# Bilinear sampling in a fused two-layer convolution: where the transposed source blocks come from

## The chip, the cores and the metric

One core of one Trainium2 chip runs the whole program. Its engines are named as in the profile: PE (TensorE, matrix multiplication, with PEld for its weight loads), DVE (VectorE), ACT (ScalarE), POOL (GpSimd) and SP (SyncE, which only issues DMAs here). The metric is the device time of one execution in microseconds; lower is better.

## The reference

The input has 32 images of 96 channels and 56 x 56 pixels, all in float32. Layer 0 expands to 576 channels, applies a 3 x 3 depthwise convolution, squeeze-and-excite and a projection back to 96 channels, and adds its input. Layer 1 gates that result by channel and by pixel to y, and samples y at learned offsets. The part that this document is about, cut to what matters:

```
y = x * ca * sa
offset = _conv(aux, off_w, off_b, (1, 1))      # aux: y, 4 coordinates, a frequency map
y_base = _conv(y, base_w, base_b, (1, 1))
px, py = xx + off[:, :, 0], yy + off[:, :, 1]  # 9 taps for every pixel
sampled = _grid_sample_taps(y, px, py)         # bilinear, zero outside
y_def = jnp.einsum('bcthw,oct->bohw', sampled, def_w.reshape(c, c, 9)) + def_b
z = (1 - gate) * y_base + gate * y_def         # then batch norm over all images, + x, relu
```

## The kernel before, in words

The images go through three stages that overlap: `hidden` (layer 0 up to the depthwise convolution, stored to `h2d`), `attend` (projection from `h2d` with the `hq` loads of L307 and the matmuls of L323, spectra, and the two gates `ca` and `sa`), and the sampling of an image. The main loop of `layers` walks the sampling in 224 bands of 8 rows, 7 for each image. While the bands of image b run, the generator `attend` of image b+1 and `hidden` of image b+2 are advanced step by step (`pump`), so that their work lies between that of the sampling. A band has 17 slots: one for each of its 14 tiles of 4 columns and three at its end. Work that must come some slots later is put into the list `later` with a slot number, and `pump` calls it then.

The gated image stands in one buffer `yp` in SBUF (channels on partitions, two rows and columns of padding). It is refilled for image b+1 row by row behind the bands of image b: `refill` loads 38 rows at band 5 (`turn`), and more at the ends of bands 5 and 6; `attend_rows` multiplies by the gates four slots later.

Sampling works on tiles of 4 x 4 pixels. All bilinear taps of such a tile lie in a source block of 8 x 8 pixels (offsets are bounded by a check at the end). For each half of a band (h = 0, 1; 7 tile columns, two tiles above each other) the kernel needs

- the weights: `offsets` makes them one or two bands ahead. Its offsets go from `at` to DRAM (`od`, POOL, L634), come back spread over 112 partitions (`ht`, SP, L646), are turned to hat functions on ACT (L649, held at its place in the program, and L650), and are stored as `hd` (ACT's queue, L653). `weights_load` then loads, on SP, the column factors `wc` and the row factors `wr` of a half, each as two DMAs of 64 partitions x 4,032 bytes whose source has an outer dimension of 8 (a broadcast of 8 copies or 8 rows), L664 and L665. `weights` multiplies them on DVE (L671). `prepare` loads one half ahead of the multiplication.
- the source blocks with pixels on partitions: `block_channels` copies the 14 blocks of 8 x 8 pixels out of `yp` on POOL (L682, two copies), transposes them one tile column at a time on PE (L686, seven transposes of 96 x 128), and copies the two PSUM banks to `yt` on ACT (L688, two copies).

`sample_tiles` multiplies block by weights (L700, 28 matmul records for a half, in a group of 3 and one of 4 tile columns), ACT copies the result to `v` (L704), `pack` moves taps 7 and 8 under the others (L711, three copies), and `deform` applies the 3 x 3 kernel (L719) after the first group of the next half.

SP issues its DMAs in the order of the program. The order on the other engines is worked out by the compiler from the dependencies and its own estimate of times, apart from instructions that are held at their place. Every DMA of SP and of ACT's queue signals on one of 8 semaphores taken in turn, so that the ninth DMA waits until the first has landed.

Of the kernel before, what the change touches and what calls it, by code (L numbers as in the profile page):

```python
# [7 lines left out]
FP = mybir.dt.float32  # L8
# [8 lines left out]
C, H, W = 96, 56, 56  # L17
# [3 lines left out]
RB = 8  # L21
# [9 lines left out]
PD = 2  # L31
HY, WY = H + 2 * PD, W + 2 * PD
# [4 lines left out]
TS = 4  # L37
NTX = W // TS
NTH = NTX // 2
TP = TS * TS  # L40
GROUPS = ((0, 3),), ((3, 5), (5, 7))
REACH = PD
SB = TS + 2 * REACH
NS = SB * SB
KP = NTAP * TP
BC = 64
# [16 lines left out]
AHEAD = 1  # L63
READY = 1
# [50 lines left out]
def bank(p):  # L115
    return p["mm"].tile([128, 512], FP, name="mm")
# [441 lines left out]
def load_rows(nc, p, yp, b, x1, r0, r1):  # L558

    rows = yp[:C, PD + r0 : PD + r1, PD : PD + W]  # L560
    nc.sync.dma_start(rows, x1.rearrange("c (h w) -> c h w", h=H)[:, r0:r1])
    sab = p["q2"].tile([C, RB, W], FP, name="sab")[:, : r1 - r0]
    nc.gpsimd.dma_start(sab, p["sa", b].rearrange("o (h w) -> o h w", h=H)[:, r0:r1].to_broadcast([C, r1 - r0, W]))
    return rows, sab


def attend_rows(nc, p, b, rows, sab):

    nc.vector.scalar_tensor_tensor(rows, rows, p["ca", b], sab, ALU.mult, ALU.mult)
# [49 lines left out]
def offsets(nc, p, yp, j, top, hids, ybs, hds):  # L619
# [22 lines left out]
    for _ in range(4):  # L642
        yield
    ht = p["ht"].tile([SB * NTX, 4, KP], FP, name="ht")
    src = od.rearrange("t s o p -> t (s o p)").unsqueeze(0).to_broadcast([SB, NTX, 4 * KP])
    nc.sync.dma_start(ht.rearrange("q n k -> q (n k)"), src)  # L646
# [4 lines left out]
    yield  # L651
    hd = p["dp"].tile([4, SB, NTX, KP], FP, name="hd")
    nc.scalar.dma_start(hd.rearrange("x i t n -> (i t) x n"), ht)  # L653
# [3 lines left out]
def weights_load(nc, p, hd, h):  # L657

    src = hd.rearrange("n i t k -> n i (t k)")[:, :, h * NTH * KP : (h + 1) * NTH * KP]
    wc = p["wc"].tile([2 * NS, NTH * KP], FP, name="wc")  # L660
    wr = p["wr"].tile([2 * NS, NTH * KP], FP, name="wr")
    for s in range(2):
        ps = slice(s * NS, (s + 1) * NS)
        nc.sync.dma_start(wc[ps], src[2 * s].unsqueeze(0).to_broadcast([SB, SB, NTH * KP]))  # L664
        nc.sync.dma_start(wr[ps], src[2 * s + 1].unsqueeze(1).to_broadcast([SB, SB, NTH * KP]))  # L665
    return wc, wr


# [3 lines left out]
    return wc  # L672


def block_channels(nc, p, yp, j, h):

    yt = p["yt"].tile([2 * NS, NTH, C], FP, name="yt")
    yb = p["ybl"].tile([C, NTH, 2, SB, SB], FP, name="ybl")
    src = yp[:C, j * RB : j * RB + SB, h * NTH * TS : h * NTH * TS + SB]
    for s in range(2):  # L680
        blocks = bass.AP(src.tensor, src.offset + s * TS * WY, [src.ap[0], [TS, NTH], [WY, SB], [1, SB]])
        nc.gpsimd.tensor_copy(yb[:, :, s], blocks)  # L682
    for lo, hi in ((0, 4), (4, NTH)):
        pt = bank(p)
        for t in range(lo, hi):
            nc.tensor.transpose(pt[:, (t - lo) * C : (t - lo + 1) * C], yb[:, t].rearrange("c s r x -> c (s r x)"),  # L686
                                p["w"]["ident"][:C, :C])
        nc.scalar.copy(yt[:, lo:hi].rearrange("p t c -> p (t c)"), pt[:, : (hi - lo) * C])  # L688
    return yt


def sample_tiles(nc, p, yt, s, v, group):
# [3 lines left out]
    for (lo, hi), pt in zip(group, pts):  # L696
        for t in range(lo, hi):
            for k in range(2):
                ps = slice(k * NS, (k + 1) * NS)
                nc.tensor.matmul(pt[k][:C, (t - lo) * KP : (t - lo + 1) * KP], yt[ps, t], s[ps, t * KP : (t + 1) * KP],  # L700
# [174 lines left out]
    w["thT"], w["twT"], w["tv"], w["thM"] = thT, twT, tv, thM  # L875


def padded(nc, p, a, images):

    cp = p["cp"]  # L880
    yps = [cp.tile([CJ, HY, WY], FP, name=f"yp{i}") for i in range(images)]
    for t in yps:
        nc.gpsimd.memset(t, 0.0)
        nc.sync.dma_start(t[C : C + 4, PD : PD + H, PD : PD + W], a["coord"])
        nc.sync.dma_start(t[CA:, PD : PD + H, PD : PD + W], a["place"])
    p["s4"] = [cp.tile([H, 3, WP], FP, name=f"s4_{i}") for i in range(2)]
    for t in p["s4"]:
        nc.gpsimd.memset(t, 0.0)
    return yps
# [8 lines left out]
def layers(tc, a, dp, x1d, zd, stats, far):  # L898
# [6 lines left out]
    nc = tc.nc  # L905
    B = x1d.shape[0]
    with ExitStack() as ctx:
        p = {"tc": tc, "dp": ctx.enter_context(tc.tile_pool(name="l1d", bufs=3, space=DRAM))}
        pools(tc, ctx, p, PSUM, (("mm", 6), ("acc", 1), ("pd", 1)))
        hidden_constants(tc, ctx, a, p)  # L910
        constants(tc, ctx, a, p)
        yp, = padded(nc, p, a, 1)
        top = p["cp"].tile([NOFF, NBD + 1], FP, name="top")
        nc.gpsimd.memset(top, 0.0)
        pools(tc, ctx, p, None, (("xt", 2), ("acch", 2), ("pl", 2), ("w3s", 1), ("hq", 9), ("o", 2), ("x2", 3),
                                 ("ca", 2), ("s1p", 1), ("xc", 2), ("sp", 1), ("sq", 1), ("q1", 2), ("q2", 2), ("hid", 3), ("yb", 4),
                                 ("off", 1), ("st", 2), ("ht", 1), ("wc", READY + AHEAD + 1), ("wr", AHEAD + 1), ("yt", 2), ("ybl", 1),
                                 ("vp", 2)))

        def first(b):  # L920
# [13 lines left out]
        streams, later = [], []  # L934
        slot = 0

        def flush():
            while later:
                later.pop(0)[1]()

        held = {}
        count = lambda it: sum(1 for _ in it)
# [5 lines left out]
        due = 0.0  # L948
# [38 lines left out]

        filled = {}

        def refill(b, upto):  # L990

            upto = min(H, upto)
            r = filled.get(("y", b), 0)
            while ("sa", b) in p and r < upto:
                r1 = min(upto, r + RB)
                args = load_rows(nc, p, yp, b, x1d[b], r, r1)
                later.append((slot + 4, lambda args=args: attend_rows(nc, p, b, *args)))
                r = filled["y", b] = r1
            r = filled.get(("fq", b), 0)
            if ("fq", b) in p and r < upto:  # L1000
                load_freq(nc, p, yp, b, r, upto)
                filled["fq", b] = upto
# [21 lines left out]
        def fill():  # L1024
            for r in range(RB, H + 1, RB):
                refill(0, r)
                flush()
                yield

        for _ in beside(fill()):  # L1030
            pass
        bands = [(b, j) for b in range(B) for j in range(NBD)]
        hids, ybs, hds, ready = [], [], [], []

# [8 lines left out]
        flush()  # L1043
        p.pop("diag")
        n_loads = 0
        loads = []

        def prepare(upto):

            nonlocal n_loads  # L1050
            while n_loads < min(upto, 2 * len(hds)):
                n, m = divmod(n_loads, 2)
                loads.append(weights_load(nc, p, hds[n], m))
                n_loads += 1

        prepare(READY + AHEAD)
        for _ in range(READY):
            ready.append(weights(nc, *loads.pop(0)))
        yts = [block_channels(nc, p, yp, 0, 0)]
        start(0, turn * (NTX + 2))  # L1060
        for n, (b, j) in enumerate(bands):
            if j == 0:
                st = p["st"].tile([C, NBD, 6], FP, name="st")
            if j == turn:
                drain()
                refill(b + 1, j * RB - PD)
                flush()
                start(b + 1, slots)
            more = find(n + 2) if n + 2 < len(bands) else iter(())
            next(more, None)  # L1070
            for h in range(2):
                v = p["vp"].tile([128, NTAP, NTH, 2, TP], FP, name="v")
                prepare(2 * n + h + READY + AHEAD)
                s = ready.pop(0)
                yt = yts.pop(0)
                for i, group in enumerate(GROUPS):
                    sample_tiles(nc, p, yt, s, v, group)
                    for _ in range(group[0][0], group[-1][1]):
                        next(more, None)
                        pump()  # L1080
                    if i == 0:
                        for end in ends:
                            end()
                        ends.clear()
                        if h == 1 and n + 1 < len(bands):
                            yts.append(block_channels(nc, p, yp, bands[n + 1][1], 0))
                        ready.extend(weights(nc, *ws) for ws in loads[:1])
                        del loads[:1]
                        if h == 0:
                            yts.append(block_channels(nc, p, yp, j, 1))  # L1090
                pack(nc, v)
                if h == 0:
                    gate = gate_of(nc, p, hids[n])
                ends.append(lambda n=n, h=h, v=v, gate=gate, st=st: end_half(n, h, v, gate, st))
            for _ in more:
                pass
            pump()
            pump()
            pump()
            if b + 1 < B:  # L1100
                refill(b + 1, (j + 1) * RB - PD if j < NBD - 1 else H)
            if j == NBD - 1:
                nc.vector.tensor_reduce(top[:, NBD:], top, AX.X, ALU.max)
# [4 lines left out]
        every = p["cp"].tile([NOFF, 1], FP, name="every")  # L1108
# [344 lines left out]
```

## Time and profile before

| quantity | value |
|---|---|
| time, median of 3 runs (lowest to highest) | 9753.98 us (9741.36 to 9758.91) |
| the profiled execution: its span, the only time the page gives of it | 9792.0 us |
| PE, DVE, ACT, POOL busy | 90%, 74%, 55%, 27% of the span |
| mean granted TensorE clock | 0.937 |
| DMA traffic | 1485.54 MB in 1,085,590 packets |
| share of the 16 DMA engines: SP's queue q1, ACT's queue q10, POOL's q0 | 39.0%, 9.1%, 6.3% |

The span runs from the first to the last instruction and is 38 us (0.4%) longer than the median of the runs. Group rows of the profile read: line, engine, operation, out<-in by the names of the program, shapes, count, then busy time in us and mean ns of one, then idle time of the engine just before them. A matmul in float32 has two records; a transpose has one. A mean on PE is the time from start to end of one record, which overlap; what one adds to the path is less.

### The profile page before, as it was taken

To read this page: it belongs to the slowest core of one execution; us is meant where nothing else is said; L and a number is where in the kernel's file an instruction comes from. 1 tells how busy PE (TensorE), PEld (TensorE's weight loads), DVE (VectorE), ACT (ScalarE), POOL (GpSimd) and SP (SyncE) were. 2 spreads that over 40 slices of the span, in tenths; PEclk is the share of its full clock that TensorE was granted. 3 is DMA by queue.
4 is the path that set the end of the run, shared out by engine and by line. 5 is a ranking of instruction groups with operands and counts; after the bars stand their busy time and mean duration, and the time that the engine had idled before them with its cause. 6 is when DMAs were issued, how large, how long until landed. Compare 5 with 4: busy or idle time off the path is not lost. (4 is left out here: it accounts for less than half of the span.)

```text
span 9792.0 us, 122438 instructions
## 1 busy us (share of the span) xinstructions
PE 8810.8 (90%) x43766; PEld 5029.2 (51%) x43766; DVE 7212.9 (74%) x6948; ACT 5381.4 (55%) x10262; POOL 2646.4 (27%) x2639
## 2 busy tenths in 40 slices
PE   6899999999999999999999999999999999999970
PEld 3455555555555555555555555555555555555540
DVE  6687777777777777877777877777787777778323
ACT  2355555555555555555555555555556555555453
POOL 1122223322222332232333222233223223322210
PEclk9889999999999999999999999999999999999985
DMA  3345555555555554555555455555555555555549
GB/s 94 106 123 150 148 154 158 149 143 139 148 151 152 157 152 135 142 154 150 154 151 150 133 147 148 150 153 151 138 149 148 153 153 156 150 139 144 132 147 417
DMA packets 1085590, 1485.54 MB, mean 152 GB/s; under 512 B 606671, under 2 KB 856223, under 8 KB 1072687
## 3 DMA queue, kind: packets, MB, share of 16 engines
q1 hardware_dynamic: 875011, 985.23, 39.0%
q10 hardware_dynamic: 153675, 329.79, 9.1%
q0 software_dynamic: 56288, 162.60, 6.3%
q8 instruction: 352, 5.77, 0.3%
q14 instruction: 264, 2.15, 0.1%
HBM read 1064.28 MB, written 412.65 MB: 151 GB/s over the span
## 5 line engine op out<-in xcount | busy, mean ns | idle before, releaser
L259 DVE SCALAR_TENSOR_TENSOR acch<-hp,w,acch 128x1512 f32<-128x1512 f32 (+1 forms) x2250 | 4264.4, 1895 | 33.4
L682 POOL COPY ybl<-yp 96x448 f32<-96x448 f32 x896 | 1107.4, 1263 | 2047.5 <-PE mm L686 2047.0
L582 PE MATMUL mm<-yp,c_jointW 104*128 104x448 f32 x4032 | 1643.7, 560 | 6.2 <-DMA yp<-fqd 3.5
L719 PE MATMUL pd<-v,c_def 128*96 128x224 f32 (+1 forms) x6272 | 1435.4, 379 | 175.6 <-ACT v L711 152.9
L719 PEld LDWEIGHTS pd<-v,c_def 128*96 128x96 f32 (+1 forms) x6272 | 1055.9, 174 | 472.6 <-ACT v L711 187.2
L700 PE MATMUL mm<-wc,yt 64*96 64x144 f32 x12544 | 1138.6, 298 | 148.7 <-ACT hp L170 54.4
L582 PEld LDWEIGHTS mm<-yp,c_jointW 104*128 104x128 f32 x4032 | 782.8, 196 | 799.0 <-issue 734.2
L166 PE MATMUL mm<-xt,w 96*128 96x392 f32 (+3 forms) x2688 | 1105.2, 549 | 73.8 <-ACT yt L688 39.8
L323 PE MATMUL mm<-hq,w3s 128*96 128x392 f32 (+1 forms) x2560 | 1029.1, 541 | 118.2 <-DMA hq<-h2d 101.9
L671 DVE TENSOR_TENSOR wc<-wc,wr 128x1008 f32<-128x1008 f32 x448 | 560.7, 1252 | 767.0 <-DMA wr<-hd 597.5
L700 PEld LDWEIGHTS mm<-wc,yt 64*96 64x96 f32 x12544 | 863.8, 160 | 487.7 <-issue 219.5
L704 ACT COPY v<-mm 96x288 f32<-96x288 f32 (+1 forms) x2688 | 999.5, 440 | 180.1 <-PE mm L700 136.4
L170 ACT ACTIVATE hp<-mm,sh,inv 128x392 f32<-128x392 f32 (+2 forms) x1216 | 815.9, 673 | 242.0 <-PE mm L166 171.3
L611 PE MATMUL mm<-yp,c_base0W 96*64 96x448 f32 x4032 | 915.5, 551 | 0.0
L219 ACT ACTIVATE acch<-acch,sh,inv 128x1568 f32<-128x1568 f32 x288 | 487.6, 1693 | 660.5 <-DVE acch L259 646.6
L711 ACT COPY v<-v 32x448 f32<-32x448 f32 x1344 | 755.1, 562 | 29.7
L634 POOL DMA_DIRECT2D od<-at x224 | 185.9, 830 | 2045.3 <-DVE at L630 1510.0
L323 PEld LDWEIGHTS mm<-hq,w3s 128*96 128x96 f32 (+1 forms) x2560 | 403.3, 173 | 651.4 <-issue 492.9
L443 POOL TENSOR_TENSOR o<-o,xc 96x392 f32<-96x392 f32 x256 | 394.9, 1542 | 994.5 <-ACT o L325 992.5
L397 PE MATMUL mm<-s,c_GV 112*112 112x464 f32 x1536 | 662.9, 573 | 0.0
L688 ACT COPY yt<-mm 128x384 f32<-128x384 f32 (+1 forms) x896 | 351.5, 441 | 531.0 <-PE mm L686 527.7
L166 PEld LDWEIGHTS mm<-xt,w 96*128 96x128 f32 (+1 forms) x2688 | 370.3, 184 | 485.4 <-issue 304.2
(191 smaller groups left out, 8924.6 us busy)
## 6 DMA issues: line engine op xcount, KB each, us to landing
h2d<-acch ACTq DMA_DIRECT2D x288, 784.0 KB
wc<-hd SPq DMA_DIRECT2D x896, 252.0 KB
wr<-hd SPq DMA_DIRECT2D x896, 252.0 KB
hq<-h2d SPq DMA_DIRECT2D x1024, 196.0 KB
x<-x1d SPq DMA_DIRECT2D x768, 98.0 KB
ht<-od SPq DMA_DIRECT2D x224, 252.0 KB
hd<-ht ACTq DMA_DIRECT2D x224, 252.0 KB
xt<-in_x SPq DMA_DIRECT2D x64, 609.0 KB
```

The lines of the kernel that those rows point to most:

```text
L166: nc.tensor.matmul(pt[p0 : p0 + w1.shape[1], : rows * W], w1, xts[hf][:, r0 * W : (r0 + rows) * W], start=True, stop=True)
L170: nc.scalar.activation(h1[lo:hi, row0 : row0 + rows, 1 : 1 + W], pt[lo:hi, : rows * W].rearrange("p (h w) -> p h w", h=rows), AF.Silu, bia ...
L259: nc.vector.scalar_tensor_tensor(acc[:, lo:hi], win, wk, acc[:, lo:hi], ALU.mult, ALU.add)
L323: nc.tensor.matmul(pt[:C, :EW], w3s[ps, ch], hq[ps], start=(i == 0), stop=(i == NCH - 1))
L397: nc.tensor.matmul(pt[: 2 * W, :n].rearrange("p (q u) -> p q u", q=NPB), w["GV"][:, g], m, start=(k == 0), stop=(k == 1))
L582: nc.tensor.matmul(view, weights[:, k], yp[:channels, r0 : r0 + RB, dx + PD - 1 : dx + PD - 1 + W], start=(k == 0), stop=(k == NTAP - 1))
L611: nc.tensor.matmul(pb[k % 2 * BC : (k % 2 + 1) * BC, :BW].rearrange("p (h w) -> p h w", h=RB), w["base"][:, k], yp[:C, r0 : r0 + RB, dx + ...
L682: nc.gpsimd.tensor_copy(yb[:, :, s], blocks)
L700: nc.tensor.matmul(pt[k][:C, (t - lo) * KP : (t - lo + 1) * KP], yt[ps, t], s[ps, t * KP : (t + 1) * KP], start=True, stop=True)
L704: nc.scalar.copy(v[:C, :, lo:hi, k].rearrange("c k t p -> c t k p"), pt[k][:C, : (hi - lo) * KP].rearrange("c (t k p) -> c t k p", t=hi - ...
L711: nc.scalar.copy(v[C:, 1 + 2 * i : 3 + 2 * i], v[i * QC : (i + 1) * QC, KA:])
L719: nc.tensor.matmul(out.rearrange("c q (t x) -> c t q x", x=TS), p["w"]["def"][ks, k], v[ks, k].rearrange("c t s (r x) -> c t (s r) x", r=T ...
```

## The change

The copies of blocks on POOL and the transposes of blocks are taken out. Instead, each group of up to 8 rows of the gated image is transposed once, some slots after it was gated (`turn_rows`): four PE transposes (one for each column modulo 4, a strided read of 120 pixels of 96 channels), one ACT copy from PSUM to `yq`, and one DMA on POOL's queue that stores it to a DRAM tensor `turned` of the shape [4, 60, 15, 96] (column modulo 4, row, column div 4, channel), one such tensor for even and one for odd images. Padding rows of the two tensors are written once at the start. `prepare` then issues, after the four weight loads of a half, four more DMAs on SP (`block_load`), each with 32 partitions x 2,688 bytes out of 4 columns x 8 rows of `turned`. Pixels now stand in `yt` by column first and row second, so `wc` and `wr` swap their two broadcast dimensions. `yt` has three buffers in place of two, `ybl` is gone, and `yq` has one. `flush` can now leave what was newly appended while it runs. The core of the diff:

```
 def weights_load(nc, p, hd, h):
...
-        nc.sync.dma_start(wc[ps], src[2 * s].unsqueeze(0).to_broadcast([SB, SB, NTH * KP]))
-        nc.sync.dma_start(wr[ps], src[2 * s + 1].unsqueeze(1).to_broadcast([SB, SB, NTH * KP]))
+        nc.sync.dma_start(wc[ps], src[2 * s].unsqueeze(1).to_broadcast([SB, SB, NTH * KP]))
+        nc.sync.dma_start(wr[ps], src[2 * s + 1].unsqueeze(0).to_broadcast([SB, SB, NTH * KP]))
...
-def block_channels(nc, p, yp, j, h):
+def turn_rows(nc, p, yp, yT, r0, r1):
+
+    n = (r1 - r0) * NTY
+    every = yp[:C, PD + r0 : PD + r1].rearrange("c h w -> c (h w)").rearrange("c (n x) -> c x n", x=TS)
+    pt = bank(p)
+    for x in range(TS):
+        nc.tensor.transpose(pt[:n, x * C : (x + 1) * C], every[:, x], p["w"]["ident"][:C, :C])
+    yq = p["yq"].tile([RB * NTY, TS, C], FP, name="yq")
+    nc.scalar.copy(yq[:n].rearrange("p x c -> p (x c)"), pt[:n, : TS * C])
+    nc.gpsimd.dma_start(yT[:, PD + r0 : PD + r1].rearrange("x h t c -> (h t) x c"), yq[:n])
+
+
+def block_load(nc, p, yT, j, h):
 
     yt = p["yt"].tile([2 * NS, NTH, C], FP, name="yt")
-    yb = p["ybl"].tile([C, NTH, 2, SB, SB], FP, name="ybl")
-    src = yp[:C, j * RB : j * RB + SB, h * NTH * TS : h * NTH * TS + SB]
     for s in range(2):
-        blocks = bass.AP(src.tensor, src.offset + s * TS * WY, [src.ap[0], [TS, NTH], [WY, SB], [1, SB]])
-        nc.gpsimd.tensor_copy(yb[:, :, s], blocks)
-    for lo, hi in ((0, 4), (4, NTH)):
-        pt = bank(p)
-        for t in range(lo, hi):
-            nc.tensor.transpose(pt[:, (t - lo) * C : (t - lo + 1) * C], yb[:, t].rearrange("c s r x -> c (s r x)"),
-                                p["w"]["ident"][:C, :C])
-        nc.scalar.copy(yt[:, lo:hi].rearrange("p t c -> p (t c)"), pt[:, : (hi - lo) * C])
+        for g in range(2):
+            r0, t0 = j * RB + s * TS, h * NTH + g
+            q0 = s * NS + g * TS * SB
+            nc.sync.dma_start(yt[q0 : q0 + TS * SB], yT[:, r0 : r0 + SB, t0 : t0 + NTH])
     return yt
...
+        def attended(b, args, r, r1):
+            attend_rows(nc, p, b, *args)
+            later.append((slot + 4 + r // TS, lambda: turn_rows(nc, p, yp, turned[b % 2], r, r1)))
+
...
                 loads.append(weights_load(nc, p, hds[n], m))
+                b, j = bands[n]
+                yts.append(block_load(nc, p, turned[b % 2], j, m))
...
-                        if h == 1 and n + 1 < len(bands):
-                            yts.append(block_channels(nc, p, yp, bands[n + 1][1], 0))
                         ready.extend(weights(nc, *ws) for ws in loads[:1])
                         del loads[:1]
-                        if h == 0:
-                            yts.append(block_channels(nc, p, yp, j, 1))
```

More of the change, by code (lines that the diff above doesn't have):

```diff
@@ L43 @@
 SB = TS + 2 * REACH
+NTY = WY // TS
 NS = SB * SB
@@ L875, in constants, with padded @@
     w["thT"], w["twT"], w["tv"], w["thM"] = thT, twT, tv, thM
-def padded(nc, p, a, images):
+def padded(nc, p, a, images, turned=()):
     cp = p["cp"]
@@ L883, in padded @@
         nc.gpsimd.memset(t, 0.0)
+        for yT in turned:
+            for n in (0, PD + H):
+                nc.sync.dma_start(yT[:, n : n + PD].rearrange("x h t c -> x (h t c)"), t[:TS, : C // 2].rearrange("x h w -> x (h w)")[:, : PD * NTY * C])
         nc.sync.dma_start(t[C : C + 4, PD : PD + H, PD : PD + W], a["coord"])
@@ L911, in layers @@
         constants(tc, ctx, a, p)
-        yp, = padded(nc, p, a, 1)
+        turned = [dp.tile([TS, HY, NTY, C], FP, name=f"turned{i}") for i in range(2)]
+        yp, = padded(nc, p, a, 1, turned)
         top = p["cp"].tile([NOFF, NBD + 1], FP, name="top")
@@ L916, in layers @@
                                  ("ca", 2), ("s1p", 1), ("xc", 2), ("sp", 1), ("sq", 1), ("q1", 2), ("q2", 2), ("hid", 3), ("yb", 4),
-                                 ("off", 1), ("st", 2), ("ht", 1), ("wc", READY + AHEAD + 1), ("wr", AHEAD + 1), ("yt", 2), ("ybl", 1),
+                                 ("off", 1), ("st", 2), ("ht", 1), ("wc", READY + AHEAD + 1), ("wr", AHEAD + 1), ("yt", 3), ("yq", 1),
                                  ("vp", 2)))
@@ L935, in layers, with flush @@
         slot = 0
-        def flush():
-            while later:
-                later.pop(0)[1]()
+        def flush(rest=True):
+            due, later[:] = later[:], []
+            for _, end in due:
+                end()
+            if rest and later:
+                flush()
         held = {}
@@ L996, in refill @@
                 args = load_rows(nc, p, yp, b, x1d[b], r, r1)
-                later.append((slot + 4, lambda args=args: attend_rows(nc, p, b, *args)))
+                later.append((slot + 4, lambda args=args, r=r, r1=r1: attended(b, args, r, r1)))
                 r = filled["y", b] = r1
@@ L1026, in fill @@
                 refill(0, r)
-                flush()
+                flush(False)
                 yield
@@ L1031, in layers @@
             pass
+        flush()
         bands = [(b, j) for b in range(B) for j in range(NBD)]
@@ L1045, in layers @@
         n_loads = 0
-        loads = []
+        loads, yts = [], []
         def prepare(upto):
@@ L1058, in layers @@
             ready.append(weights(nc, *loads.pop(0)))
-        yts = [block_channels(nc, p, yp, 0, 0)]
         start(0, turn * (NTX + 2))
@@ L1066, in layers @@
                 refill(b + 1, j * RB - PD)
-                flush()
+                flush(False)
                 start(b + 1, slots)
```

## The prediction

> **What bounds the kernel now.** I read the page's busy rows by slice first, then the waits, then the groups of the lines that the change touches, and last windows over single bands.
>
> ```profile
> PE   6899999999999999999999999999999999999970
> ...
> PEclk9889999999999999999999999999999999999985
> DMA  3345555555555554555555455555555555555549
> ```
>
> From the fourth slice on PE is 90% busy or more in every slice, so the path is PE's own order of work plus the moments when it waits. Between the 7th and the 217th band (8,555 us) the records leave PE 518 us idle, 2.5 us of each 40.7 us band. The DMA row is an average over 16 engines and looks harmless. The waits:
>
> ```profile
> ACT yt L688 <- PE mm L686: 527.7, 269, 4.6
> ...
> ACT ht L649 <- DMA ht<-od: 347.1, 107, 9.0
> ```
>
> ```profile
> PE pd L719 <- ACT v L711: 152.9, 71, 4.6
> PE mm L323 <- DMA hq<-h2d: 101.9, 56, 6.3
> ...
> PE mm L166 <- ACT yt L688: 39.8, 23, 3.2
> ```
>
> The first answer is of all engines, the second of PE; columns: total us, times, longest. PE hardly waits for blocks; it waits for ACT's `v` and for `hq`. ACT in turn stands still for the landing of `ht`. How the first grows out of the second shows the timeline of a band's second half:
>
> ```profile
> 5009.41 0.78 ACT L649 ACTIVATE ht<-ht,c_blk 112x576 f32<-112x576 f32 x1 [1.27 <-DMA ht<-od]
> ...
> 5010.22 0.56 ACT L711 COPY v<-v 32x448 f32<-32x448 f32 x1
> ...
> 5010.83 1.43 PE L719 MATMUL pd<-v,c_def 128*96 128x224 f32 x3 [2.02 <-ACT v L711]
> ```
>
> The `v` copy stood behind `ht` on ACT, so a late landing became 2.02 us of idle PE. And `ht` stands on SP directly behind a weight burst:
>
> ```profile
> 5655.71 0.61 SPq L665 DMA_DIRECT2D wr<-hd  x1
> 5656.37 0.57 SPq L664 DMA_DIRECT2D wc<-hd  x1
> 5656.98 0.57 SPq L665 DMA_DIRECT2D wr<-hd  x1
> 5657.66 0.66 SPq L646 DMA_DIRECT2D ht<-od  x1
> ```
>
> Last, bands 4, 5 and 6 of one image as windows; the last two columns are the DMA share and GB/s:
>
> ```profile
> 5559.90:5594.80 34.90, 32.36 (x184) 19.87 (x183) 28.90 (x26) 20.69 (x39) 10.01 (x9) 0.95 0.57 142
> 5594.80:5629.80 35.00, 34.99 (x167) 19.22 (x166) 20.75 (x18) 17.66 (x38) 11.84 (x12) 0.95 0.52 137
> 5629.80:5684.10 54.30, 49.26 (x199) 24.41 (x199) 33.21 (x28) 25.80 (x45) 17.59 (x22) 0.94 0.83 223
> ```
>
> In band 6, where the next image is projected from `hq`, the engines are 83% busy on average.
>
> **What is removed.**
>
> ```profile
> L682 POOL COPY ybl<-yp 96x448 f32<-96x448 f32 x896 | 1107.4, 1263 | 2047.5 <-PE mm L686 2047.0
> ...
> L686 PE MATMUL mm<-c_ident,ybl 96*128 96x96 f32 x3136 | 350.6, 248 | 11.4 <-ACT sq L399 6.3 <-POOL ybl L682 5.1
> ...
> L688 ACT COPY yt<-mm 128x384 f32<-128x384 f32 (+1 forms) x896 | 351.5, 441 | 531.0 <-PE mm L686 527.7
> ```
>
> PE: the mean of 248 ns is start to end; by how much each record moves PE's end forward, the 3,136 transposes cost 276.5 us, 88 ns each. The new ones are 4 for each of 255 row groups (there are 255 `sab` loads, one per group): 1,020 x 88 = 90 us. Net 187 us. The strided read is in no row: should its weight load double from the 141 ns of the old one and nothing hide that, it costs 144 us more, at best nothing; weight loads run beside the matmuls here, so I take nothing. Waits of PE that end on these lines go as well: 39.8 + 0.4 on `yt`, 11.4 before L686, 52 us. ACT: 896 copies, 395 us, become 255 of about 477 ns (the row of 128x384), 122 us. ACT is 55% busy, so this counts only where PE waits for `v`: 71 times at most 0.78 us (two copies), 55 us; I take half, 28. POOL's 1,107 us of copies cost nothing now (PE waited 5.1 us for them) and give nothing back, but for DVE's ease beside them, which is off the path. Sum: 187 + 52 + 28 = 267 us, 8.3 us for each of 32 images.
>
> **What is added, off the path.** The store of `yq`: 255 DMAs on POOL's queue, 480 rows of 384 B. The nearest issue, `od` with 504 rows, takes 830 ns; POOL is 27% busy and loses four copies per band. It waits there for the ACT copy, with `od`, `sab` and `zd` behind it; POOL's `od` already waits up to 29 us for DVE. Its packets lie between 224 B (mean 18 ns) and 576 B (33 ns): 122,400 x 25 ns over 16 engines is 190 us, 6 us per image. The first rows are turned some 6 slots into band 5 and first loaded at the middle of band 6, 25 slots in, so SP doesn't wait for the store. Swapping the broadcasts of `wc` and `wr` leaves number and size as they are: 0. The padding stores lie in the prologue.
>
> **What is added, on the path: four DMAs of 32 x 2,688 B per half, on SP between the weights and `ht`.** Data first: 344 KB beside 1,032 KB of weights, which take 8.8 us (median, first packet to last). Spread alike that is +2.9 us of transfer. But the Trainium skill ("DMA: Bandwidth & Descriptors", Rules for kernel authors, and "Why a DMA increments its semaphore by 16 and not by 1") says that a DMA uses as many engines as the largest k up to 16 that divides the slowest dimension of both sides, the lowest-numbered ones. The trace bears it out for k = 8: of the weights' 4,032 B packets (source outer dimension 8) exactly 8 are under way in 62% of their time and more than 9 in 1%; and q1 has 54,267 packets of 4 bytes, the completion writes, for 4,555 SP DMAs, where 8 for `wc`, `wr` and `ht`, 14 for `x` and 16 for `hq` sum to about 54,200 (16 for the weights would give 68,500). The new source is [4, 8, 672], so k = 4; no run here shows k = 4 yet. Each of these four engines then moves 32 packets per half, not 8. Price of a packet: at the rate of `hq`'s 1,568 B (median 66 ns) 113 ns, at the mean of the weights' 4,032 B (246 ns) 164 ns; between them `ht`'s 2,304 B (mean 135 ns), the nearest, gives 157. I take 150: 4.8 us per half (3.6 to 5.2), against 1.2 if 16 engines shared.
>
> Now where that falls. With k as above, the four engines carry some 221 us of packets in a 285 us image (any packet at all is under way for 224). Added are 14 x 4.8 + 6 = 73 us: 294, more than the 277 that PE needs after the saving. It fits nowhere without stalls:
> - Band 6: already full. Of 9.6 us I take 7 as PE idle (`hq` late: q2, q4 and q6 of the projection have 2.4, 4.8 and about 0 us to spare).
> - Bands 0 and 4: ACT reaches `ht` 9.4 and 9.0 us after its issue and gets it at 11.5 and 10.7; PE idles 2.6 and 2.5 us for it. Another 4.8 us each: 9.6.
> - Bands 3 and 5: ACT reaches it at 12.5 and 5.6 us; PE is covered by the two 3 x 3 convolutions (11 us). 1 us each, 2 together; without that cover 4.8 each.
> - Bands 1 and 2: `ht` has 20 us. Nothing.
> - The clock: after PE idle of 2 us and more (bands 0, 1, 4, 6) 5.2 to 5.5 us run at half clock, in other bands 0 to 0.5 (band 3: 3.9 after 1.9 us). Three longer stalls, 1 us each: 3 (bounds 0 and 5).
> - The loads themselves: blocks land about 4.8 us after the weights, which land 11 to 35 us ahead of their use in twelve of an image's fourteen halves, and 3.3 and 2.4 us ahead in band 6, in the 7 above.
>
> Sum per image: 7 + 9.6 + 2 + 3 - 8.3 = +13.3 us if none of it overlaps. A stall in one band lets the queue catch up for the next, and ACT's order is planned anew; I strike 2. +11.3 x 32 = +362 us on a span of 9,792, 10,154; the runs stand 38 us under the span, so about 10,120.
>
> **Rivals.** (1) The loads are hidden, as the row averages say (DMA share 0.5): the DMA is spread over 16 engines or the packets are cheap, and `ht` comes less than 2 us later. Then the sum is -8.3 us per image plus a rest in band 6 of 0 to 6: 9,490 to 9,700, say 9,600. For it: 12 of 14 halves have time to spare. Against it: the count of completion writes. It decides at +8 us of stalls per image, an `ht` about 2.5 us later. (2) The four engines become the bound: 301 us per image at the upper price, and no better filled than 93%: 323 us, +38 per image, about 10,950. For it: band 6. Against it: bands 1 to 3 have 10 to 20 us of room. (3) SP waits for the turned rows: 8 stores per image, 6 us each where `zd`'s landing shows 6.1, +48 us per image at worst; the 60 us of lead speak against it, and I hold it in (2)'s chance.
>
> **Chances.** Slower by stalls, likeliest: 0.63, own range 9,850 to 10,480. Saturated or blocked: 0.11. Slower by little: 0.03. Within 0.2%, about what a measurement can tell from no change: 0.04. Faster: 0.19. So slower 0.77. The range 9,640 to 10,500 leaves out the saturated case and the better part of the faster one, about 0.19.
>
> **What would show it.** L686, L682 and L688 gone; about 1,020 transposes; PE's advance on them 90 us. Packets of 2,688 B: 57,344 on q1, never much more than 4 under way, mean near 150 ns. ACT's wait for `ht` from 347 to about 1,000 us, PE's for `v` L711 and `hq` more than doubled, PE busy below 88%, clock below 0.937. If more than 4 such packets run at once, or ACT's wait for `ht` stays below 500 us, the forecast is wrong and rival 1 holds.

## The result and the profile after

The changed kernel takes 10,160.9 us (median of 4 runs, 10,124.1 to 10,169.3) against 9,756.4 us on the same chip: a ratio of 1.040, 95% interval 1.0378 to 1.0422. It is slower, and 41 us above the predicted 10,120. The profiled execution has a span of 10,153.1 us (before: 9,792.0) at a granted clock of 0.913 (before: 0.937).

One sentence ahead of the prediction must be put right. `refill` runs at the end of every band from the end of band 2 on, not from band 5; so the first rows of the next image are turned in band 3. This matters below.

The same three rows of the page as before:

```profile
PE   6889998989998899999999889999999988999970
...
PEclk9889999999999999999899999999999999998985
DMA  2345555555555555555555555555555555555549
```

PE now stands between 80% and 90% in ten of the 40 slices (before: in one), and two more slices have a lower clock. The DMA row has hardly changed, although 195 MB more are moved (1,485.54 to 1,681.03 MB). The average over 16 engines does not show the cost. The groups of the two turned steps (busy us, mean ns, then the idle time ahead and what ended it):

```profile
L682 PE MATMUL mm<-c_ident,yp 96*120 96x96 f32 x1020 | 168.9, 296 | 14.6 <-DVE yp L570 14.6
...
L684 ACT COPY yq<-mm 120x384 f32<-120x384 f32 x255 | 121.9, 478 | 208.5 <-DMA turned<-yq 194.1 <-PE mm L398 6.2 <-PE mm L167 5.9
```

The counts and ACT's 122 us are as forecast. By how much each record moves PE's end forward, the transposes cost 132.6 us, 130 ns each (before: 88). The last column was not forecast: ACT stands 194 us for the store of `yq` to land, since `yq` has one buffer. The waits of all engines, and of PE (total us, times, longest):

```profile
ACT ht L650 <- DMA ht<-od: 527.1, 124, 9.6
...
ACT yq L684 <- DMA turned<-yq: 194.1, 83, 7.5
```

```profile
PE mm L377 <- DMA x<-x1d: 191.7, 29, 8.7
PE mm L324 <- DMA hq<-h2d: 121.8, 64, 8.0
PE mm L583 <- DMA yp<-fqd: 113.2, 28, 5.7
PE mm L377 <- POOL x L357: 104.8, 32, 5.9
PE mm L707 <- DMA yt<-turned: 98.3, 56, 7.6
PE mm L167 <- ACT yq L684: 91.4, 28, 5.1
...
PE pd L726 <- ACT v L718: 20.8, 64, 1.0
```

ACT waits longer for `ht` than before (347 to 527 us), but PE's wait for `v` behind it has all but gone (152.9 to 20.8). ACT's order explains that: a `v` copy followed `ht` directly in 68 of 224 bands before, and does in 11 now. In its place stand waits that PE hardly had before: the spectra's loads `x` (L377), a frequency map (`fqd`, ahead of the 3 x 3 convolution L583), the blocks, and the first layer's matmuls (L167) behind the `yq` copy. Four of the waits come 28 to 32 times, about once an image. The waits for `x`, for POOL's `x` (L357) and for `fqd` were small before (PE waits of before):

```profile
PE mm L376 <- POOL x L356: 14.3, 20, 3.4
...
PE mm L376 <- DMA x<-x1d: 8.4, 3, 7.0
...
PE mm L582 <- DMA yp<-fqd: 3.5, 1, 3.5
```

The two spans differ by 361 us. PE's records divide it into 326 us more idle time (between the first and the last record), 144 less for the transposes, and about 180 more for all other PE work, whose instructions are the same. That last part is the clock: an image ran 26.7 us at half clock before and runs 42.4 us so after. Of PE's work, 812 us ran at half clock before and 1,221 us after, and half of the difference is 205 us. Over the fourteen kernels of this document the other work takes 0.47 us longer for each us of PE's work at half clock (correlation 0.98). The table shows where (mean of 30 images, us):

| place | idle before | idle after | ended by, after | half clock before | after |
|---|---|---|---|---|---|
| band 0, second half | 3.1 | 7.3 | `x` 6.0 | 5.2 | 11.8 |
| band 3, second half | 1.9 | 6.3 | `yq` 3.1, POOL's `x` (L357) 3.0 | 3.9 | 9.9 |
| band 4, second half | 2.9 | 4.0 | `fqd` 3.8 | 5.5 | 6.2 |
| band 6, both | 4.7 | 6.9 | `hq` 3.8, `yt` 2.8 | 5.7 | 7.7 |

The part of band 3's wait that ends on `yq` is a chain through three engines. Timelines of PE, ACT and POOL in one such place:

```profile
3364.50 1.86 PE L167 MATMUL mm<-xt,w 96*128 96x448 f32 x2 [3.91 <-ACT yq L684]
```

```profile
3363.97 0.48 ACT L684 COPY yq<-mm 120x384 f32<-120x384 f32 x1 [2.43 <-DMA turned<-yq]
...
3368.76 0.47 ACT L684 COPY yq<-mm 90x384 f32<-90x384 f32 x1 [0.27 <-DMA turned<-yq]
```

```profile
3358.07 0.85 POOL L685 DMA_DIRECT2D turned<-yq  x1
3358.94 1.77 POOL L357 TENSOR_TENSOR x<-x,sa 112x448 f32<-112x448 f32 x1
3364.74 0.83 POOL L685 DMA_DIRECT2D turned<-yq  x1 [4.03 <-ACT yq L684]
```

Band 3 turns three groups (8, 8 and 6 rows), planned two slots apart. POOL issues the first store at 3358.07, it lands some 5.8 us later, and only then may ACT overwrite `yq` at 3363.97. Its PSUM bank stays full until then, and PE stands 3.91 us for it. Over all 255 stores the time from issue to landing is 2.8 to 9.1 us, median 5.9.

### The profile page after: what moved, and what is told of

Its sections match the earlier page's. It is cut to its first block, busy times and chain, and to the rows that moved or that the text cites. A ratio compares the mean times of both kernels' runs of the same rounds, so it can differ in the third digit from the quotient of the medians.

```text
span 10153.1 us, 119404 instructions
## 1 busy us (share of the span) xinstructions
PE 8846.9 (87%) x41650; PEld 4918.1 (48%) x41650; DVE 7111.7 (70%) x6948; ACT 5162.8 (51%) x9621; POOL 1776.6 (17%) x1998
## 2 busy tenths in 40 slices
DMA packets 1165451, 1681.03 MB, mean 166 GB/s; under 512 B 618637, under 2 KB 868654, under 8 KB 1152542
## 5 line engine op out<-in xcount | busy, mean ns | idle before, releaser
L260 DVE SCALAR_TENSOR_TENSOR acch<-hp,w,acch 128x1512 f32<-128x1512 f32 (+1 forms) x2250 | 4214.5, 1873 | 30.0
L583 PE MATMUL mm<-yp,c_jointW 104*128 104x448 f32 x4032 | 1834.0, 609 | 113.2 <-DMA yp<-fqd 113.2
L726 PE MATMUL pd<-v,c_def 128*96 128x224 f32 (+1 forms) x6272 | 1362.2, 367 | 39.8 <-ACT v L718 20.8
L583 PEld LDWEIGHTS mm<-yp,c_jointW 104*128 104x128 f32 x4032 | 833.1, 212 | 968.6 <-issue 942.4
L707 PE MATMUL mm<-wc,yt 64*96 64x144 f32 x12544 | 1121.5, 297 | 119.7 <-DMA yt<-turned 98.3
L167 PE MATMUL mm<-xt,w 96*128 96x392 f32 (+3 forms) x2688 | 1109.1, 555 | 131.6 <-ACT yq L684 91.4
L726 PEld LDWEIGHTS pd<-v,c_def 128*96 128x96 f32 (+1 forms) x6272 | 1030.6, 169 | 322.5 <-issue 87.1
L324 PE MATMUL mm<-hq,w3s 128*96 128x392 f32 (+1 forms) x2560 | 1050.4, 552 | 123.4 <-DMA hq<-h2d 121.8
L377 PE MATMUL mm<-c_FU,x 112*112 112x116 f32 x3072 | 460.0, 302 | 319.4 <-DMA x<-x1d 191.7
L444 POOL TENSOR_TENSOR o<-o,xc 96x392 f32<-96x392 f32 x256 | 440.2, 1719 | 1523.1 <-ACT o L326 1520.4
L377 PEld LDWEIGHTS mm<-c_FU,x 112*112 112x112 f32 x3072 | 413.7, 206 | 444.8 <-issue 124.4
L167 PEld LDWEIGHTS mm<-xt,w 96*128 96x128 f32 (+1 forms) x2688 | 363.2, 182 | 508.0 <-issue 325.6
```

What stands on the lines that cost most here:

```text
L167: nc.tensor.matmul(pt[p0 : p0 + w1.shape[1], : rows * W], w1, xts[hf][:, r0 * W : (r0 + rows) * W], start=True, stop=True)
L260: nc.vector.scalar_tensor_tensor(acc[:, lo:hi], win, wk, acc[:, lo:hi], ALU.mult, ALU.add)
L324: nc.tensor.matmul(pt[:C, :EW], w3s[ps, ch], hq[ps], start=(i == 0), stop=(i == NCH - 1))
L377: nc.tensor.matmul(pt[: 2 * W, i * 4 * V : (i + 1) * 4 * V], x2s[g][:, 2 * i : 2 * i + 2, :].rearrange("h c w -> h (c w)"), w["FU"], start ...
L583: nc.tensor.matmul(view, weights[:, k], yp[:channels, r0 : r0 + RB, dx + PD - 1 : dx + PD - 1 + W], start=(k == 0), stop=(k == NTAP - 1))
L726: nc.tensor.matmul(out.rearrange("c q (t x) -> c t q x", x=TS), p["w"]["def"][ks, k], v[ks, k].rearrange("c t s (r x) -> c t (s r) x", r=T ...
```

## The experiments

**Theory T** is the prediction's: the loads cost what they do since each lies on four DMA engines. **Rival A**: the 1,792 loads cost as such, by their issue on SP, their slots (8 semaphores) and completions. **Rival B**: PE's waits for the blocks themselves. **Theory C**: the rest of the change takes back its own saving, through the single `yq` buffer or a new order of work. Four engines is what the records show: q1's 4-byte completion writes rise from 54,267 to 61,451, by 7,184, four for each load (and 16 for the prologue's padding). Exactly four of the 2,688 B packets are under way in half of their time, more than four in 6%; their mean is 121.5 ns.

| run | what differs from the changed kernel | us, median | ratio to before, 95% interval |
|---|---|---|---|
| away4 | loads into an unread tile, 4 engines | 10,129.6 | 1.0376 to 1.0424 |
| away8 | the same, 8 engines | 9,953.7 | 1.0181 to 1.0239 |
| away16 | the same, 16 engines | 10,076.5 | 1.0299 to 1.0361 |
| away16c | 16 engines, source rows apart | 10,073.0 | 1.0285 to 1.0343 |
| noload | no block loads after the first three | 9,795.5 | 1.0032 to 1.0079 |
| small | loads of 2 KB in place of 84 KB | 9,669.4 | 0.9876 to 0.9945 |
| spread | row groups four slots apart | 9,922.6 | 1.0128 to 1.0198 |
| nlsp | noload and spread | 9,644.1 | 0.9844 to 0.9912 |
| k16 | two block copies in DRAM, 16 engines | 10,093.4 | 1.0307 to 1.0379 |
| k8 | eight planes in DRAM, 8 engines | 10,071.5 | 1.0287 to 1.0336 |
| k8sp | k8 and spread | 9,960.8 | 1.0175 to 1.0221 |
| away8sp | away8 and spread | 9,719.3 | 0.9939 to 0.9974 |

k8, k8sp and away16c ran on another chip than the rest of the table; the kernel before takes 9,768 us there, 16 more than the 9,752 beside most of the others.

### The number of engines alone: away4, away8, away16

```
-    yt = p["yt"].tile([2 * NS, NTH, C], FP, name="yt")   # and its four loads
+    # the sampling reads p["held"][0], loaded once; in every half:
+    yd = p["yt"].tile([2 * NS, NTH * C], FP, name="yd")
+    for k in range(4):   # away8: [[1552, 8], [336, 4], ...]; away16: [[380, 32], ...]
+        nc.sync.dma_start(yd[k * 32 : k * 32 + 32], bass.AP(src.tensor, src.offset, [[HW, 4], [336, 8], [1, NTH * C]]))
```

> The changed kernel, except that the sampling reads one block loaded once (so its output is left wrong) and the four loads per half go to a tile that nobody reads, from the input instead of the turned rows, with the same outer source dimension of 4, the same 32 rows of 2,688 B. It takes away PE's wait for the blocks, nothing else. Theory (the time is lost on four DMA engines): within 1.5% of the changed kernel, 10,000 to 10,250. Rival A (the loss is the eight more DMAs per band on SP and their semaphore turns): the same here. Rival B (PE waits for the blocks themselves): below 9,850.

> As away4 in number, bytes, place and order of every instruction, but the source has an outer dimension of 8: the rows spread over 8 engines. (The sampling reads one block, as in away4.) Theory: 2.4 instead of 4.8 us per half on the loaded engines, so about half of the loss is back: 9,800 to 9,950. Rival A: as away4 within 0.5%.

> As away4, but with an outer dimension of 32, so 16 engines. (The sampling reads one block, as in away4.) Theory: 1.2 us per half on every engine, 9,600 to 9,800, faster than the kernel before or level with it. Rival A: as away4 within 0.5%. Rival C (the rest of the change, the single yq buffer or the new order on the engines, costs the time): above 9,950.

These three have the same order of work on PE, ACT and DVE, so nothing but the loads differs. away4 falls into T's range and 31 us below the changed kernel though nobody waits for its loads: rival B is out as the main cost. PE's wait for the blocks (98.3 us) has gone, but its wait for `hq` has doubled from 121.8 (PE waits of away4); the loads harm what shares the DMA with them:

```profile
PE mm L324 <- DMA hq<-h2d: 239.3, 84, 7.2
```

Going from four to eight engines takes off 176 us, with the same bytes and the same number of loads; that is T's mechanism, measured alone (4 us above its range). Sixteen engines miss T's range by 277 us. The time lies in rival C's range (above 9,950) and just below A's. All sixteen are in use (q1 has 21,504 completions more than away4, twelve for each load), but a packet takes 218.9 ns on average where it took 127 on eight and 121 on four, and seldom are more than 8 under way. So T's premise for sixteen, packets at the old price, was wrong.

### Why sixteen are not better: away16c

```
-            [[380, 32], [1, NTH * C]]
+            [[NTH * C, 32], [1, NTH * C]]
```

> The run with the unread loads on sixteen engines once more (the sampling reads one block held from the start), but with source rows that lie apart, 2,688 bytes each, one after the other in the input, in place of rows that overlapped at a stride of 1,520 bytes. If the overlapping source made those packets slow (219 ns against 127 on eight engines): packets of 120 to 140 ns now and 9,800 to 9,950. If it is the sixteen engines writing to the same 32 partitions that makes them slow: packets of 200 to 230 ns again and 10,030 to 10,110.

The packets take 221.4 ns, the run 10,073.0 us. The overlapping source was not the reason. The 32 shared partitions are not the main one either, as the records of away16 show: a load packet that starts while no weight packet (4,032 B) is under way takes 146 ns, and one that starts beside seven or more of them takes 299 ns. The second kind is 43% of the packets on sixteen engines and 1% on eight (580 of 57,472), where the loads seldom meet the weights and a packet without them takes 122 ns. The weights' own packets are slower too, 255 ns against 226. Why the two slow each other down stays open, and so does the rest, 146 against 122. The Trainium skill's rule to use all 16 engines ("DMA: Bandwidth & Descriptors", Rules for kernel authors) did not pay for these loads: eight are 123 us better (away8 against away16), though sixteen are 53 us better than four.

### The loads taken away: noload, small

```
-            nc.sync.dma_start(yt[q0 : q0 + TS * SB], yT[:, r0 : r0 + SB, t0 : t0 + NTH])
+            if first:          # three held blocks; noload issues nothing after them
+                nc.sync.dma_start(yt[q0 : q0 + TS * SB], yT[:, r0 : r0 + SB, t0 : t0 + NTH])
+            else:              # small only
+                nc.sync.dma_start(yt[q0 : q0 + TS * SB, 0, :16], yT[:, r0 : r0 + SB, t0, :16])
```

> The changed kernel with the block loads left out after the first three (the sampling reads those three blocks in turn, so the output is wrong); turning and storing stay. Theory: all of the loss is gone and the saving shows, 9,450 to 9,600. Rival C: above 9,950.

> As the run without block loads (9,795 us), but each later load is still issued, in its place and number, and moves only 32 pieces of 64 bytes into a held block that the sampling reads; the blocks themselves are left out, so the sampled values are those of the first three. Theory T (the price of the loads is the 2,688-byte packets that lie on four DMA engines): hardly any bytes are left, so 9,760 to 9,860. Rival A (the price is the 1,792 loads as such: their issue on SyncE, their slots and completions): the time stays near that of the changed kernel, 10,080 to 10,200.

noload is T's clear miss, and no hit for rival C (above 9,950): with all loads gone the kernel is still no faster than before (ratio 1.0056). The saving of 267 us that the prediction counted does not appear. Its PE waits name what stands against it (PE waits of noload):

```profile
PE pd L731 <- ACT v L723: 229.7, 76, 5.4
PE mm L167 <- ACT yq L684: 176.8, 29, 6.7
```

The `yq` wait has nearly doubled and PE's wait for `v` is back at more than its old size: as before, a `v` copy follows `ht` directly in 68 bands. small, with every load issued but hardly any bytes, is 126 us faster still (91 us below T's range), though it does strictly more than noload. Its `v` copies follow `ht` in 68 bands too, but ACT waits half as long for `ht`. ACT's waits for `ht` in noload, then in small, and PE's for `v` in small:

```profile
ACT ht L650 <- DMA ht<-od: 385.2, 113, 8.3
```

```profile
ACT ht L650 <- DMA ht<-od: 189.4, 72, 7.0
```

```profile
PE pd L733 <- ACT v L725: 66.2, 86, 3.1
```

The compiler's order of work differs as well (966 of ACT's 9,621 records stand elsewhere), and no run separates the order from the times at which SP issues. So two versions whose orders differ may be some 126 us apart for that alone.

small also answers rival A. SP does stand for slots in the changed kernel (SP waits):

```profile
SPq L695 <- DMA hd<-ht: 480.4, 63, 10.8
...
SPq L647 <- DMA h2d<-acch: 375.3, 59, 8.0
```

Neither line needs `hd` or `h2d`; ACT's stores hold the semaphores that come next in turn. All such waits of SP sum to 121 us before and 1,480 after. But small has 960 us of them at 9,669 us, and away8sp (below) 1,359 us at 9,719, while k8sp has 577 us at 9,961. They do not set the time. small issues all the loads and lies 411 us below A's range, so A is out as the main cost.

### The row groups further apart: spread, nlsp

```
-            later.append((slot + 4 + r // TS, lambda: turn_rows(nc, p, yp, turned[b % 2], r, r1)))
+            later.append((slot + 4 + r // 2, lambda: turn_rows(nc, p, yp, turned[b % 2], r, r1)))
```

> The changed kernel, with the row groups of a chunk turned four slots apart instead of one, so that the only buffer of a turned group (ScalarE waited 194 us for its store, TensorE 91 us behind it) is free when the next group comes. Theory C (the single buffer takes back a good part of what the transposes save): the 91 us of TensorE's wait and some clock go, 10,000 to 10,080. Theory T alone (only the block loads matter): TensorE will wait for loads instead, 10,120 to 10,200.

> The run without block loads (9,795 us; all loads after the first three are left out, so the sampled values are wrong from there on) with the row groups turned four slots apart. Theory C: its 177 us of TensorE's wait for the single buffer go and the saving of the transposes shows: 9,580 to 9,660. Against it (the stall is only moved, to the next thing that is late, such as the copies of the sampled values on ScalarE): 9,740 to 9,830.

The groups of a chunk stand two slots apart in the changed kernel (the expectations say one, which was a slip of mine) and four in these two runs. That number takes off 238 us with the loads (77 us below C's range) and 151 us without them (in C's range). Theory C holds, and for more than the 91 us of PE's `yq` wait that I had counted. The edit also delays the groups of the later bands, by 6 to 14 slots, and the compiler's order changes with it. But of the 7.3 us that an image loses in spread, 5.0 lie in the second half of band 3, where three groups follow each other; away8sp loses 4.9 there against away8 and nlsp 4.5 against noload. A second buffer for `yq`, which would have asked the same without moving any work, was not run. The waits of ACT and of PE in spread:

```profile
ACT yq L684 <- DMA turned<-yq: 29.0, 11, 5.3
```

```profile
PE mm L377 <- DMA x<-x1d: 178.3, 26, 8.4
PE mm L324 <- DMA hq<-h2d: 123.3, 63, 6.6
PE mm L583 <- DMA yp<-fqd: 120.2, 28, 5.6
PE mm L707 <- DMA yt<-turned: 73.0, 55, 7.5
PE mm L377 <- POOL x L357: 71.1, 48, 3.5
```

PE's wait for `yq` is gone from the list; the other stalls are as they were or somewhat shorter. PE's idle time falls by 83 us, and its work takes 145 us less with the same instructions: an image has 31.9 us at half clock, not 42.4, and the second half of band 3 has 4.1, not 9.9. So the larger part of what the stalls cost here is the slower clock behind them. In nlsp the wait for `v` stays as the longest (PE waits of nlsp):

```profile
PE pd L731 <- ACT v L723: 245.0, 70, 6.3
```

### Versions that sample the true blocks: k16, k8, k8sp

```
 # k16: turned[i] as [7, TS, 8, NTY, C] for i in (0, 1): 8-row blocks, begun at row 0 and at row 4
-            nc.sync.dma_start(yt[q0 : q0 + TS * SB], yT[:, r0 : r0 + SB, t0 : t0 + NTH])
+            nc.sync.dma_start(yt[q0 : q0 + TS * SB], yT[s][j].rearrange("x r t c -> (x r) t c")[:, t0 : t0 + NTH])
```

```
 # k8: turned as [2 * TS, HY, NTY, C]; every group is stored twice, the second time one tile to the left
+    for g in range(2):
+        n0 = (PD + r0) * NTY - g
+        nc.gpsimd.dma_start(flat[g * TS : (g + 1) * TS, n0 : n0 + n].rearrange("x n c -> n x c"), yq[:n])
...
+        nc.sync.dma_start(yt[s * NS : (s + 1) * NS], yT[:, r0 : r0 + SB, t0 : t0 + NTH])   # two loads a half
```

> The changed kernel, but the turned image is held in DRAM as two sets of blocks, so that the source of a block load is one run of 32 rows and the load goes over 16 engines, not four; bytes and packets of the loads are the same, the stores of the turned rows are made twice (GpSimd issues two to four stores for a group instead of one). Theory T: the loads cost what two packets at each engine cost, and the time comes down to 9,820 to 9,980 (the run on eight engines took 9,954). Rival A (number of loads, not engines): 10,130 to 10,250, since stores are added.

> The changed kernel with eight planes in DRAM instead of four (plane 4+x is plane x shifted by one tile, so every turned group is stored twice by GpSimd), and a half's block comes in two loads of 64 rows over eight engines instead of four loads of 32 rows over four: the same packets of 2,688 bytes, half as many loads. Theory T (number of engines): as the run on eight engines against that on four, which gained 176 us, less something for the second stores: 9,960 to 10,060. Rival A (the bytes, on whatever engines): 10,110 to 10,200.

> The eight planes and the row groups turned four slots apart together. If the two costs add (238 us came off with the spacing alone): the time of the eight planes alone less 180 to 240, so 9,740 to 9,860, as fast as the kernel before (9,752) at best. If both take away the same stalls: 9,880 to 9,930, as the spacing alone (9,923).

All three miss every range set for them. k16 gains 68 us where T wanted 180 or more; its packets take 207.9 ns, slow as in the other runs on 16 engines. k8 gains 89 us and lies 12 above T's range: its packets are quick (130.4 ns), but two stores hold `yq` longer. PE waits of k8:

```profile
PE mm L167 <- ACT yq L684: 236.8, 29, 9.6
PE mm L324 <- DMA hq<-h2d: 188.3, 61, 6.7
```

k8sp takes the wait for `yq` out of the list, and the waits for `v` and `hq` take its place; it stays 38 us above spread. Its `v` copies follow `ht` directly in 67 bands (11 in the changed kernel), and ACT waits 599 us for `ht`. PE waits of k8sp:

```profile
PE pd L727 <- ACT v L719: 250.3, 122, 5.6
PE mm L324 <- DMA hq<-h2d: 201.1, 59, 7.8
```

### Both causes taken away: away8sp

Its edit is that of away8 and that of spread together.

> The run with the unread loads on eight engines (the sampling reads one block held from the start, so its values are not those of the image) and the row groups turned four slots apart; the stores are made once, as in the changed kernel. If the two costs add, as theory T and theory C together have it: 9,954 less 150 to 240, so 9,720 to 9,810, level with the kernel before. If spacing and engines take away the same stalls: 9,880 to 9,930.

9,719.3 us, 1 us below the range: the two costs add (234 us for the spacing on eight engines; 238 on four), and a kernel with all the loads and all the stores of the change is 0.4% faster than before. Its blocks are not the image's, though, and PE waits for none of them. No version that samples the true blocks came below 9,922.6 us.

## Why the prediction came out near, and where it was wrong

The sum was right within 41 us, and that was luck: the cost of the loads, put too high, stood in for a cost that was missed and for a saving that did not come in full. One chain of runs from before to after divides the difference:

| term | forecast | measured | from |
|---|---|---|---|
| the saving | -267 | -108 | before 9,752 to nlsp 9,644 |
| the block loads, with what waits behind them | +629 | +279 | nlsp to spread 9,923 |
| row groups that follow each other too closely | 0 | +238 | spread to changed 10,161 |
| sum | +362 | +409 | |

The division depends on the path: by way of noload (9,795) in place of spread, the spacing costs 151 and the loads 365. Each of these steps also changes the compiler's order, so some 126 us of each may be order. What is safe is that both costs are there and large: the spacing was worth 238, 234, 151 and 111 us in four pairs, the engine count 176 us at one and the same order. The size of the saving is not safe, nor which of the two costs is the larger.

- **Four engines**: right. The count of completions, four packets under way and away8 show it. The price was near: 121.5 ns a packet, against 150 taken. One sum behind it was told short: `wc`, `wr`, `ht`, `x` and `hq` have 47,360 completions, not 54,200; the rest is from SP's other 491 DMAs. The conclusion stands, as 16 for the weights would have added 14,336.
- **Where the lateness falls**: "Bands 0 and 4: ACT reaches `ht`" was wrong as a path. `ht` did come later, but ACT's new order has a `v` copy directly behind it in 11 bands, not 68, and PE's `v` wait fell to 20.8 us. The prediction said that ACT's order would be planned anew, and struck 2 us an image; the new order did away with most of this path. The late ones were other loads, `x` in band 0, `fqd` in band 4, `hq` and `yt` in band 6. The forecast for band 6, 7 us for one image, was also too high: idle rose there by 2.2 us.
- **The mark "ACT's wait for `ht` from 347 to about 1,000"**: 527, barely above the 500 that I had set as refuting it. PE's waits for `v` and `hq` "more than doubled": 21 and 122. PE busy below 88% and a clock below 0.937: met (87%, 0.913).
- **"What is added, off the path. The store of `yq`"**: the step that failed most. I asked who waits on POOL for the store, and whether SP waits for the rows; I did not ask who waits for the buffer that it reads. One buffer, a store of 5.9 us (median) and a next group two slots later, some 5 us (119 slots in an image of 296 us), make a stall, and the trace of before could not show it. 151 to 238 us were costed at nothing. The store's price was off too, without effect: its packets are mostly of 4,224 B (6,720 of them, 242 ns each), not rows of 384 B, and take 136 us of 16 engines, not 190. My wrong reading of `refill` hid it further: it put the groups into bands 5 and 6, where I was counting other things.
- **The saving**: 1,020 transposes at 130 ns, not 88 (43 us less saved). The PE work itself fell by 213 us from before to nlsp, but 91 us came back as idle time, since PE then waits longer for `v` (152.9 to 245.0) and `hq` (101.9 to 143.0). The prediction had 28 us less wait for `v`.
- **The clock**: put at 3 us an image, 96 us in all. PE's unchanged work took about 180 us longer. That term was mis-sized. The two stalls that grew most, by 4.2 us in band 0 and 4.4 in band 3, each brought 6 to 7 us more at half clock.
- **Rival 1** (hidden, 9,600): its premise, loads over 16 engines, gives 10,073 to 10,093 here. **Rival 2** (four engines saturated, 10,950): not near. **Rival 3** (SP waits for turned rows): no wait of SP ends on their store. Its relative, ACT waiting for that store, is the cost that was missed.

## What to carry to other kernels

For every buffer that a step fills and a DMA then reads, set the time until that DMA lands against the time until the next fill; a store "off the path" is on it as soon as its only buffer is. Count on how many engines a load's shape puts it, and look for the victims among all loads that share those engines, not only the one behind it in the queue. And when a forecast comes out right, look at its terms one by one: here an oversized cost stood in for one that was missed.

## What the runs showed of the hardware that I had not expected

- In this kernel, loads of 32 rows of 2,688 B into 32 partitions did best on eight engines: 121 ns a packet on four, 127 on eight, 208 to 221 on sixteen with three kinds of source. On sixteen, 43% of the packets start beside seven or more packets of the weights, and those take 299 ns (away16).
- Within this kernel the clock can cost more than the stall. With 83 us less idle time (spread) the same PE instructions were 145 us quicker.
- SP can stand 1,480 us in all for semaphores that another queue's stores hold, and the time does not follow it: 1,359 us at 9,719 (away8sp), 577 us at 9,961 (k8sp).
- A kernel that does more can be quicker by 126 us (small against noload). Its ACT waited 189 us for `ht`, not 385; whether the compiler's order or the issue times did it stays open.
